# Gathered rows taken in pairs into two running rows of a tile, joined at its end

## The chip, the cores and the metric

The kernel runs on one core of a Trainium2 chip. A core has five engines that run beside each other and meet at semaphores: TensorE (PE, with its weight loads shown as PEld), VectorE (DVE), ScalarE (ACT), GpSimd (POOL) and SyncE (SP). The metric is device microseconds of one execution; the figure compared is the median of several runs.

## What is computed

A graph of 3125 nodes with 256 features each and 103125 edges, which come sorted by their destination node, goes through two layers. Each layer adds a graph step and a linear attention, and then a mixture of eight experts. Cut to what the change touches:

```python
# layer 0: for each node the largest message over its incoming edges
theta_x = (x_dst - x_src) @ theta_w.T + theta_b
phi_x = x_src @ phi_w.T + phi_b
out = jax.ops.segment_max(relu(theta_x + phi_x), dst, num_segments=3125)
# layer 1: for each node the sum of a table's rows, one row for each incoming edge
h_all = jnp.einsum('ni,rio->nro', node_feats, W)      # 8 relations
agg = jax.ops.segment_sum(h_all[src, edge_types], dst, num_segments=3125)
```

The parts of a message that depend on the destination alone are taken out of the maximum, so that both layers come to this: for every node, fetch one 1 KB row of a table in HBM for each incoming edge, and combine the rows (maximum in layer 0, sum in layer 1).

## The kernel before

Nodes are put in order of their number of edges and cut into 25 tiles of 128 nodes, one node for each partition. `STEPS` (line 42) holds the rows that each tile fetches for every one of its nodes: from 45 for tile 0 down to 22 for tile 24, 814 in all. One call of `gather` (line 192; the profile shows all of them on line 193) is an indirect DMA issued by GpSimd that brings one row to each of the 128 partitions.

`edge_pass` (line 1334) does this for a list of groups of tiles. It runs twice: in layer 0 (line 1933, maximum, table `btab`, rows of 264 numbers, all 25 tiles) and in layer 1 (line 2570, sum, table `htab_f`, rows of 256 numbers, 21 tiles; the four tiles named in `EARLY` are summed apart, by `first_group` and `early`). For each tile it cuts the steps into chunks of three or four rows of equal size as far as that goes (`chunks`, line 94), takes a buffer `gt` from the ring `gp` (6 buffers in layer 0, line 1693; 5 in layer 1, line 1987), lets GpSimd gather the rows into it, and lets VectorE fold them: four rows into two by one operation on 512 numbers a partition (line 1356), two into one by one on 256 (line 1356), and the one into the tile's accumulator `acc` by one on 256 (line 1361; line 1359 for a tile's first chunk in layer 0). The accumulators come from the pool `accp` of six buffers.

Behind each chunk `edge_pass` calls jobs from the queue `bg`, as many as a credit allows that grows by 0.9 to 1.3 for each row. These jobs are the rest of the layer: attention, normalization, routing and experts of the tiles whose sums are done (`Fin0` in layer 0, `Group` in layer 1). The order of VectorE's and GpSimd's instructions is the order in which this code is written (`manual_schedule`, lines 1932 and 2568); the orders of the other engines come from a scheduler. So an operation on VectorE that waits for a matrix product holds up the folding of the rows behind it, and GpSimd can only run ahead until the ring `gp` is full.

In layer 0 `seen0` (line 1616) copies a number that comes with each gathered row. In layer 1 a tile's accumulator starts with the row of the node itself: `load_init` (line 2532) brings it one tile ahead, for 16 tiles by a DMA of SyncE from a table `otab` filled earlier, and for the last five tiles in the order of the pass (3, 4, 2, 1, 0; those still in `owns`) by a gather of GpSimd. `begin1` (line 2539) calls it at the start of a tile for the tile that follows.

Between the passes the table `htab_f` is made (line 2047). While it is, `early` gathers rows of the four tiles in `EARLY`, and `add_up` (line 2106) adds a buffer of up to four rows to `sums` by one operation on up to 1024 numbers.

Of the kernel before, what the change touches and what calls it, by code (L numbers as in the profile page):

```python
# [11 lines left out]
F32 = mybir.dt.float32  # L12
# [3 lines left out]
ALU = mybir.AluOpType  # L16
# [4 lines left out]
P = 128  # L21
D = 256
# [19 lines left out]
STEPS = (45, 43, 41, 39, 38, 37, 36, 35, 35, 34, 33, 33, 32, 32, 31, 30, 30, 29, 29, 28, 27, 26, 25, 24, 22)  # L42
# [4 lines left out]
U = STEPS[0] + 1  # L47
# [7 lines left out]
GROUPS = tuple(range(a, b) for a, b in zip(CUTS, CUTS[1:])) + (range(0, 1),)  # L55
# [11 lines left out]
GROUPS1 = tuple(range(b, a) for a, b in zip(CUTS1, CUTS1[1:]))  # L67
GROUPS1 = GROUPS1[2:3] + GROUPS1[:2] + GROUPS1[3:]
# [4 lines left out]
ROW = D + NX  # L73
# [27 lines left out]
def gps_kernel(ctx: ExitStack, tc: tile.TileContext, a, out):  # L101
    nc = tc.nc
    V, S, G, PE = nc.vector, nc.scalar, nc.gpsimd, nc.tensor
# [10 lines left out]
    btab = dram.tile([NPAD, ROW], F32, name="btab")  # L114
# [77 lines left out]
    def gather(dst, table, idx):  # L192
        G.indirect_dma_start(  # L193
            out=dst, out_offset=None, in_=table, in_offset=bass.IndirectOffsetOnAxis(ap=idx, axis=0)
        )
# [758 lines left out]
    with ExitStack() as prx:  # L954
# [48 lines left out]
        for at, t in enumerate(EARLY):  # L1003
            k0 = 0
            while k0 < SOON[t]:
                k1 = k0
# [3 lines left out]
                k0 = k1  # L1010
# [197 lines left out]
        own = pre.tile([P, NV * NT], F32, name="own")  # L1208
# [109 lines left out]
    def fast():  # L1318
        fx = ExitStack()
        ek = fx.enter_context(tc.tile_pool(name="ek", bufs=1))  # L1320
        htab = dram.tile([NPAD, NX * D], F32, name="htab_f")
        otab = dram.tile([NPAD, D], F32, name="otab")
        h_rows = htab.rearrange("n (r d) -> (n r) d", r=NX)
        idx2 = ek.tile([P, NT, U], I32, name="idx2g")
        accp = fx.enter_context(tc.tile_pool(name="accp", bufs=6))
        own_i = ek.tile([P, NT], I32, name="own_i")
        soon = ek.tile([P, len(EARLY), SOONEST], I32, name="soon")
        sure = ek.tile([P, len(EARLY), SOONEST], F32, name="sure")
# [2 lines left out]
        comp = bcast_load("comp", a["comp"], 4 * NX, ek)  # L1331
        br = bcast_load("br0", a["f0_br"], NX, ek)

        def edge_pass(gp, table, wide, idx, op, bg, after, groups, most, pace, own, acc_of, aside, seen=None):


            credit = 0.0
            spill = None
            for g, tiles in enumerate(groups):
                accs = []  # L1340
                left = sum(STEPS[t] for t in tiles)
                for t in tiles:
                    acc = acc_of(t)
                    ids = idx(t)
                    for i, (k0, k1) in enumerate(chunks(STEPS[t], most)):
                        m = k1 - k0
                        gw = gp.tile([P, most, wide], F32, name="gt")
                        gt = gw[:, :, :D]
                        for k in range(k0, k1):
                            gather(gw[:, k1 - 1 - k, :], table, ids[:, U - 2 - k : U - 1 - k])  # L1350
                        if seen is not None:
                            seen(t, i, k0, k1, gw)
                        begins = i == 0 and own is None
                        while m > 1 + begins:
                            h = m // 2
                            V.tensor_tensor(gt[:, :h, :], gt[:, :h, :], gt[:, m - h : m, :], op=op)  # L1356
                            m -= h
                        if begins:
                            V.tensor_tensor(acc, gt[:, 0, :], gt[:, 1, :], op=op)
                        else:  # L1360
                            V.tensor_tensor(acc, own(t) if i == 0 else acc, gt[:, 0, :], op=op)  # L1361
                        if t == 0 and i == 3:
                            V.tensor_tensor(acc[: P // 2, :], acc[: P // 2, :], spill, op=op)

                        rate = min(max(sum(c for c, _ in bg) / left, pace[0]), pace[1])
                        left -= k1 - k0
                        credit = min(credit, 0.0) + rate * (k1 - k0) if bg else 0.0
                        aside()
                        while bg and credit > 0.0:
                            cost, job = bg.popleft()  # L1370
                            job()
                            credit -= cost
                    if t == NT - 1:

                        pj = ps_mm.tile([P, 512], F32, name="mm")
                        PE.matmul(pj[: P // 2, :D], ident[:, P // 2 :], acc, start=True, stop=True)
                        spill = ek.tile([P // 2, D], F32, name="spill")
                        S.copy(spill, pj[: P // 2, :D])
                    accs.append(acc)
                after(g, tiles, accs)  # L1380
# [184 lines left out]
        with ExitStack() as l0x:  # L1565
            l0w = l0x.enter_context(tc.tile_pool(name="l0w", bufs=1))
            idx1, slots_of, sortings = {}, {}, {}
# [123 lines left out]
            b_phi = row_load("b_phi", a["ph_b"], D, l0w)  # L1691
            V.tensor_tensor(b_gnn, b_gnn, b_phi, op=ALU.add)
# [3 lines left out]
            m0 = m0x.enter_context(tc.tile_pool(name="m0", bufs=2))  # L1696

            w_qkv = m0w.tile([P, 2, 3 * D + 2], F32, name="w_qkv")
            S.dma_start(w_qkv[:, :, : 3 * D], a["m0_qkv"].rearrange("(c p) n -> p c n", p=P))
# [2 lines left out]
            for m in range(2):  # L1702
                at = slice(3 * D + m, 3 * D + m + 1)
# [179 lines left out]
            bg = deque(staged(mix_weights(), (3.0, 1.0)))  # L1883
# [39 lines left out]
            fin, waiting = [], []  # L1923
# [7 lines left out]

            with tc.manual_schedule(engines={mybir.EngineType.DVE, mybir.EngineType.Pool}):
                edge_pass(
                    gp, btab[:], ROW, idx1.get, ALU.max, bg, after0, GROUPS, 4, (0.9, 1.3), None,
                    begin0, ahead, seen0,
                )
                while bg:
                    bg.popleft()[1]()
                f0bx.close()
# [14 lines left out]
        with tc.If(again > 0):  # L1954
# [8 lines left out]
            for ts in GROUPS:  # L1963
                k = len(ts)
# [22 lines left out]
        gp = fx.enter_context(tc.tile_pool(name="gp1", bufs=5))  # L1987
        sump = fx.enter_context(tc.tile_pool(name="sump", bufs=1))
        sums = sump.tile([P, len(EARLY), D], F32, name="sums")
        with ExitStack() as tx:  # L1990
# [168 lines left out]
        with ExitStack() as l1x:  # L2159
# [5 lines left out]
            for c in range(2):  # L2165
                d = w_lu[:, c, c * P : (c + 1) * P]
# [15 lines left out]
            fin = l1x.enter_context(tc.tile_pool(name="fin1", bufs=1))  # L2182
# [385 lines left out]
            with tc.manual_schedule(engines={mybir.EngineType.DVE, mybir.EngineType.Pool}):  # L2568
                first_group()
                edge_pass(  # L2570
                    gp, h_rows, D, lambda t: idx2[:, t, :], ALU.add, bg, lambda g, *a: after1(g + 1, *a),
                    GROUPS1[1:], 4, (0.9, 1.3), lambda t: inits[t], begin1, aside,
                )
                while bg:
                    bg.popleft()[1]()
                    flush()
# [3 lines left out]
    with tc.If(unfit < 1):  # L2580
        fast()
# [78 lines left out]
```

## Time and profile before

| what | value |
|---|---|
| median of 5 runs | 2955.13 us (2948.27 to 2980.0) |
| the profiled execution | 2942.73 us, of which the span of instructions is 2941.0 us |
| mean granted TensorE clock | 0.767 |
| busy share of the span | PE 64%, POOL 59%, DVE 43%, ACT 19% |
| first and last gather of layer 0's pass | 99.9 us, 1383.7 us |
| first row gathered early, last gather of layer 1's pass | 1500.0 us, 2853.3 us |

A row of instructions reads: line, engine, operation, what is written and read, count, then busy time and mean duration, then the idle time of the engine just before these instructions and what ended it. An engine that is idle has no instruction whose inputs and buffers are ready; the releaser named is the one that came last. All instructions of VectorE and GpSimd run in the order written. A table by stretches gives for each stretch of the span the busy time of each engine with the number of instructions in brackets, the granted clock, and the share and rate of the DMA engines.

### The profile page before, as it was taken

What the parts mean: (1) busy time and instruction counts of PE and PEld (TensorE: products, weight loads), DVE (VectorE), ACT (ScalarE), POOL (GpSimd) and SP (SyncE); (2) the same over time, 40 slices, a digit from 0 to 9 for tenths busy, and PEclk for the clock granted to TensorE, in tenths of its full rate; (3) what the DMA queues carried; (4) which work ended last, traced back from release to release, by engine and by line L of the source; (5) the groups of instructions that cost most, each with busy time, mean ns of one, the idle gap of its engine ahead of it and who ended that gap; (6) DMA issues with size and microseconds to landing.
All of it is one profiled execution on the core that took longest, in us unless ns stands there. A gap on an engine that the chain in (4) does not pass through costs nothing.

```text
span 2941.0 us, 20996 instructions
## 1 busy us (share of the span) xinstructions
PE 1885.9 (64%) x6033; PEld 1182.2 (40%) x6033; DVE 1256.1 (43%) x3537; ACT 560.2 (19%) x1275; POOL 1726.7 (59%) x1830
## 2 busy tenths in 40 slices
PE   4273667403573655176898349867886796776777
PEld 3131334202341423044443125544454464564666
DVE  8343535536323434244665343434343443343342
ACT  5121211000110101012321112212112122122233
POOL 5566666676657466655036755665666566665560
PEclk9676767655786767577999568877897898887888
DMA  6433333333323233332256632222232222232220
GB/s 191 125 86 89 90 91 101 94 107 108 93 77 105 67 96 87 90 76 76 108 205 218 198 109 76 86 88 77 85 93 87 78 84 84 86 87 74 79 82 15
DMA packets 125962, 290.09 MB, mean 99 GB/s; under 512 B 41386, under 2 KB 63982, under 8 KB 122632
## 3 DMA queue, kind: packets, MB, share of 16 engines
q0 software_dynamic: 83184, 230.02, 27.8%
q1 hardware_dynamic: 38122, 55.88, 5.5%
q10 hardware_dynamic: 4526, 2.71, 0.4%
q8 instruction: 51, 0.84, 0.1%
q14 instruction: 79, 0.65, 0.1%
HBM read 249.07 MB, written 39.41 MB: 98 GB/s over the span
## 4 chain that ended last, share of the span: by engine, by line
PE 27%; issue 8%; another core or an unknown queue 6%; DVE 5%; POOL 3%; ACT 2%; DMA 1%; DVEq 0%; ACTq 0%; POOLq 0%
PE mm L2408 10%; PE py L2439 8%; PE mm L188 6%; POOL gt L193 3%; DVE gt L1356 1%; DMA gt<-htab_f,idx2g 1%; DVE bnst L162 1%; PE mm L2302 1%; PE pt L2378 1%; PE mm L2300 1%; PE pctx L2247 1%; DVE x L2458 1%; PE py L2425 0%; DVE x L2343 0%
## 5 line engine op out<-in xcount | busy, mean ns | idle before, releaser
L193 POOL DMA_INDIRECT gt<-btab,idx x814 | 802.4, 986 | 458.4 <-issue 230.7
L193 POOL DMA_INDIRECT gt<-htab_f,idx2g x742 | 732.2, 987 | 466.8 <-DVE acc L1361 230.5
L2408 PE MATMUL mm<-xT,w 128*128 128x256 f32 (+4 forms) x1408 | 429.6, 457 | 96.8 <-issue 55.1
L2439 PE MATMUL py<-w,hT 128*128 128x256 f32 (+1 forms) x1600 | 404.5, 405 | 84.0 <-issue 43.5
L1356 DVE TENSOR_TENSOR gt<-gt 128x256 f32<-128x256 f32 (+1 forms) x767 | 410.4, 535 | 91.9 <-remote 47.3
L2439 PEld LDWEIGHTS py<-w,hT 128*128 128x128 f32 (+1 forms) x1600 | 316.9, 202 | 163.1 <-issue 85.2
L2408 PEld LDWEIGHTS mm<-xT,w 128*128 128x128 f32 x1408 | 267.4, 217 | 235.7 <-issue 167.5
L2458 DVE SCALAR_TENSOR_TENSOR x<-py,wf,x 128x256 f32<-128x256 f32 x200 | 88.0, 478 | 473.4 <-remote 197.2
L2412 ACT ACTIVATE hT<-mm,b 128x256 f32<-128x256 f32 (+4 forms) x352 | 168.6, 496 | 578.1 <-PE mm L2408 297.6
L188 PE MATMUL mm<-w_rel,xT 128*128 128x512 f32 x400 | 177.1, 601 | 10.0 <-ACT xT L183 9.5
L1532 PE MATMUL mm<-w,hT 128*128 128x256 f32 x400 | 131.6, 489 | 65.3 <-issue 45.8
L1361 DVE TENSOR_TENSOR acc<-acc,gt 128x256 f32<-128x256 f32 x371 | 158.4, 427 | 27.3 <-DVE gt L1356 12.4
L1503 PE MATMUL mm<-xT,w 128*128 128x384 f32 (+2 forms) x320 | 111.1, 513 | 81.4 <-issue 43.1
L1532 PEld LDWEIGHTS mm<-w,hT 128*128 128x128 f32 x400 | 94.1, 246 | 116.4 <-issue 75.8
L188 PE MATMUL mm<-w_qkv,xT 128*128 128x512 f32 (+1 forms) x200 | 104.9, 649 | 38.7 <-ACT vs L1751 38.2
L1863 PE MATMUL pmean<-ones,xt 128*128 128x1 f32 (+1 forms) x100 | 21.2, 316 | 156.5 <-DVE xt L171 156.5
L1503 PEld LDWEIGHTS mm<-xT,w 128*128 128x128 f32 x320 | 69.5, 242 | 122.1 <-issue 64.0
L188 PEld LDWEIGHTS mm<-w_rel,xT 128*128 128x128 f32 x400 | 75.7, 192 | 103.8 <-issue 87.9
L188 PE MATMUL pt<-w_own,xT 128*128 128x256 f32 x100 | 41.7, 552 | 116.8 <-remote 68.9
L193 POOL DMA_INDIRECT gt<-htab_f,soon x72 | 73.0, 1013 | 45.7 <-issue 19.5
L1620 DVE COPY slots<-gt 128x4 f32<-128x4 f32 (+1 forms) x214 | 37.0, 173 | 122.3 <-DMA gt<-btab,idx 118.6
L1863 PEld LDWEIGHTS pmean<-ones,xt 128*128 128x128 f32 (+1 forms) x100 | 21.8, 301 | 166.6 <-DVE xt L171 165.0
(436 smaller groups left out, 2127.9 us busy)
## 6 DMA issues: line engine op xcount, KB each, us to landing
htab_f<-hs SPq DMA_DIRECT2D x25, 1024.0 KB
gt<-btab,idx POOLq DMA_INDIRECT x814
gt<-htab_f,idx2g POOLq DMA_INDIRECT x742
w<-in_f_W_dram SPq DMA_DIRECT2D x20, 512.0 KB
ntab<-x SPq DMA_DIRECT2D x5, 640.0 KB
btab<-bs SPq DMA_DIRECT2D x5, 640.0 KB
x<-in_x_dram SPq DMA_DIRECT2D x4, 640.0 KB
otab<-xn SPq DMA_DIRECT2D x16, 128.0 KB
```

The source lines that it names most:

```text
L188: PE.matmul(ps, lhs[:, c, t * P : (t + 1) * P], w[:, c, :], start=start and c == 0, stop=stop and c == 1)
L193: G.indirect_dma_start(out=dst, out_offset=None, in_=table, in_offset=bass.IndirectOffsetOnAxis(ap=idx, axis=0))
L1356: V.tensor_tensor(gt[:, :h, :], gt[:, :h, :], gt[:, m - h : m, :], op=op)
L1361: V.tensor_tensor(acc, own(t) if i == 0 else acc, gt[:, 0, :], op=op)
L1503: PE.matmul(ph[:, :n], w1[:, i, c, f * P : (f + 1) * P], xT[:, c, at0 : at0 + n], start=(c == 0), stop=(c == 1),)
L1532: PE.matmul(py[:, i * D : (i + 1) * D], hTs[i][:, f, j * P : (j + 1) * P], w2[:, i, f, :], start=False, stop=(f == FC - 1), skip_group_che ...
L1620: V.tensor_copy(slots_of[t][:, U - 1 - k1 : U - 1 - k0], gw[:, : k1 - k0, D])
L1863: PE.matmul(pmean[0][:, c : c + 1], xt_tok[:r, t, c * P : (c + 1) * P], ones[:r, 0:1], start=(t in (1, SEEN + 1) and c == 0), stop=(t in ( ...
L2408: PE.matmul(ph[:, :n], w1s[e][:, c, f * P : (f + 1) * P], xT[:, c, at0 : at0 + n], start=(c == 0), stop=(c == 1),)
L2412: S.activation(hT[:, f, :n], ph[:, :n], AF.Gelu, bias=b1[:, e, f : f + 1])
L2439: PE.matmul(py[:r, j * D : (j + 1) * D], hT[:, f, at : at + r], w2s[e][:, f, :], start=(f == 0), stop=(f == FC - 1),)
L2458: V.scalar_tensor_tensor(d, y, wf[:r, t, e : e + 1], d, op0=ALU.mult, op1=ALU.add)
```

## The change

In `edge_pass` a tile now has two running rows, `run`, in place of one accumulator. The first two rows (in layer 1 the node's own row and the first gathered row) go straight into `run`. Every further chunk has four rows, the last one what is left, and is taken in pairs: one operation on 512 numbers adds two gathered rows to the two running rows. At the end of the tile, behind the jobs of its last chunk, one operation on 256 numbers joins the two running rows into `acc`, which is only then taken from `accp`.

```diff
-        accp = fx.enter_context(tc.tile_pool(name="accp", bufs=6))
+        accp = fx.enter_context(tc.tile_pool(name="accp", bufs=5))
...
-                    acc = acc_of(t)
+                    run = run_of(t)
+                    two = run[:, :, :D]
...
-                    for i, (k0, k1) in enumerate(chunks(STEPS[t], most)):
-                        m = k1 - k0
-                        gw = gp.tile([P, most, wide], F32, name="gt")
-                        gt = gw[:, :, :D]
-                        for k in range(k0, k1):
-                            gather(gw[:, k1 - 1 - k, :], table, ids[:, U - 2 - k : U - 1 - k])
+                    n0 = 1 if owned else 2
+                    for k in range(n0):
+                        fetch_row(run[:, 1 - k, :], k)
+                    if seen is not None:
+                        seen(t, 0, 0, n0, run)
+                    for i, k0 in enumerate(range(n0, STEPS[t], 4)):
+                        k1 = min(k0 + 4, STEPS[t])
+                        gw = gp.tile([P, 4, wide], F32, name="gt")
+                        for a in range(k0, k1, 2):
+                            b = min(a + 2, k1)
+                            at = slice(k1 - b, k1 - a)
+                            for k in range(a, b):
+                                fetch_row(gw[:, k1 - 1 - k, :], k)
+                            d = two[:, : b - a, :]
+                            V.tensor_tensor(d, d, gw[:, at, :D], op=op)
                         if seen is not None:
-                            seen(t, i, k0, k1, gw)
-                        begins = i == 0 and own is None
-                        while m > 1 + begins:
-                            h = m // 2
-                            V.tensor_tensor(gt[:, :h, :], gt[:, :h, :], gt[:, m - h : m, :], op=op)
-                            m -= h
-                        if begins:
-                            V.tensor_tensor(acc, gt[:, 0, :], gt[:, 1, :], op=op)
-                        else:
-                            V.tensor_tensor(acc, own(t) if i == 0 else acc, gt[:, 0, :], op=op)
+                            seen(t, i + 1, k0, k1, gw)
...
+                    acc = accp.tile([P, D], F32, name="acc")
+                    V.tensor_tensor(acc, two[:, 0, :], two[:, 1, :], op=op)
```

`run` has two buffers in each layer. In layer 1 `load_init` writes the own row into the `run` of the tile that follows; `add_up` takes at most two rows in one operation:

```diff
-                return accp.tile([P, D], F32, name="acc")
+                return l0w.tile([P, 2, ROW], F32, name="run", bufs=2)
...
-                inits[t] = accp.tile([P, D], F32, name="acc")
+                inits[t] = fin.tile([P, 2, D], F32, name="run", bufs=2)
                 if t in owns:
-                    gather(inits[t], h_rows, own_i[:, t : t + 1])
+                    gather(inits[t][:, 0, :], h_rows, own_i[:, t : t + 1])
                 else:
-                    nc.sync.dma_start(inits[t], otab[t * P : (t + 1) * P, :])
+                    nc.sync.dma_start(inits[t][:, 0, :], otab[t * P : (t + 1) * P, :])
...
-                    e = slice(es[k0], es[k1 - 1] + 1)
-                    V.tensor_tensor(sums[:, e, :], sums[:, e, :], gt[:, e, :], op=ALU.add)
+                    for a in range(k0, k1, 2):
+                        e = slice(es[a], es[min(a + 1, k1 - 1)] + 1)
+                        V.tensor_tensor(sums[:, e, :], sums[:, e, :], gt[:, e, :], op=ALU.add)
```

A row of biases, `b_phi`, moves to a pool that is given up earlier. The number of gathers stays as it was.

More of the change, by code (lines that the diff above doesn't have):

```diff
@@ L1332, in fast, with edge_pass @@
         br = bcast_load("br0", a["f0_br"], NX, ek)
-        def edge_pass(gp, table, wide, idx, op, bg, after, groups, most, pace, own, acc_of, aside, seen=None):
+        def edge_pass(gp, table, wide, idx, op, bg, after, groups, pace, owned, run_of, aside, seen=None):
             credit = 0.0
@@ L1342, in edge_pass, with fetch_row @@
                 for t in tiles:
-                    acc = acc_of(t)
+                    run = run_of(t)
+                    two = run[:, :, :D]
                     ids = idx(t)
-                    for i, (k0, k1) in enumerate(chunks(STEPS[t], most)):
-                        m = k1 - k0
-                        gw = gp.tile([P, most, wide], F32, name="gt")
-                        gt = gw[:, :, :D]
-                        for k in range(k0, k1):
-                            gather(gw[:, k1 - 1 - k, :], table, ids[:, U - 2 - k : U - 1 - k])
-                        if seen is not None:
-                            seen(t, i, k0, k1, gw)
-                        begins = i == 0 and own is None
-                        while m > 1 + begins:
-                            h = m // 2
-                            V.tensor_tensor(gt[:, :h, :], gt[:, :h, :], gt[:, m - h : m, :], op=op)
-                            m -= h
-                        if begins:
-                            V.tensor_tensor(acc, gt[:, 0, :], gt[:, 1, :], op=op)
-                        else:
-                            V.tensor_tensor(acc, own(t) if i == 0 else acc, gt[:, 0, :], op=op)
+                    def fetch_row(dst, k):
+                        gather(dst, table, ids[:, U - 2 - k : U - 1 - k])
@@ L1362, in edge_pass @@
                         if t == 0 and i == 3:
-                            V.tensor_tensor(acc[: P // 2, :], acc[: P // 2, :], spill, op=op)
+                            V.tensor_tensor(two[: P // 2, 0, :], two[: P // 2, 0, :], spill, op=op)
                         rate = min(max(sum(c for c, _ in bg) / left, pace[0]), pace[1])
-                        left -= k1 - k0
-                        credit = min(credit, 0.0) + rate * (k1 - k0) if bg else 0.0
+                        n1 = k1 - (k0 if i else 0)
@@ L1368, in edge_pass @@
+                        left -= n1
+                        credit = min(credit, 0.0) + rate * n1 if bg else 0.0
                         aside()
@@ L1690, in fast @@
             S.dma_start(b_mix, a["m0_bout"].rearrange("(o n) -> o n", o=1))
-            b_phi = row_load("b_phi", a["ph_b"], D, l0w)
-            V.tensor_tensor(b_gnn, b_gnn, b_phi, op=ALU.add)
             gp = l0x.enter_context(tc.tile_pool(name="gp0", bufs=6))
@@ L1696, in fast @@
             m0 = m0x.enter_context(tc.tile_pool(name="m0", bufs=2))
+            b_phi = row_load("b_phi", a["ph_b"], D, m0w)
+            V.tensor_tensor(b_gnn, b_gnn, b_phi, op=ALU.add)
             w_qkv = m0w.tile([P, 2, 3 * D + 2], F32, name="w_qkv")
@@ L1933, in fast @@
                 edge_pass(
-                    gp, btab[:], ROW, idx1.get, ALU.max, bg, after0, GROUPS, 4, (0.9, 1.3), None,
+                    gp, btab[:], ROW, idx1.get, ALU.max, bg, after0, GROUPS, (0.9, 1.3), False,
                     begin0, ahead, seen0,
@@ L2571, in fast @@
                     gp, h_rows, D, lambda t: idx2[:, t, :], ALU.add, bg, lambda g, *a: after1(g + 1, *a),
-                    GROUPS1[1:], 4, (0.9, 1.3), lambda t: inits[t], begin1, aside,
+                    GROUPS1[1:], (0.9, 1.3), True, begin1, aside,
                 )
```

## The prediction

> **What bounds the kernel now.** I began with the costliest groups of the page. The two edge passes are gathers on POOL: 814 in layer 0, 742 in layer 1.
>
> ```profile
> L193 POOL DMA_INDIRECT gt<-btab,idx x814 | 802.4, 986 | 458.4 <-issue 230.7
> L193 POOL DMA_INDIRECT gt<-htab_f,idx2g x742 | 732.2, 987 | 466.8 <-DVE acc L1361 230.5
> ```
>
> A gather is 0.99 us busy and some 0.3 us of issue: 1.28 us at best. The idle time beyond issue is split by the waits of POOL over the whole run (us in total, times, longest):
>
> ```profile
> POOL gt L193 <- issue: 449.5, 1448, 4.2
> POOL gt L193 <- DVE acc L1361: 356.7, 76, 18.8
> ```
>
> So POOL stands 357 us, in 76 pieces, because the ring of `gt` buffers is full and line 1361, a chunk's last fold, has not freed one. Why DVE is late is in its own waits:
>
> ```profile
> DVE x L2458 <- remote: 197.2, 15, 24.7
> DVE x L2458 <- PE mm L2408: 136.6, 11, 25.7
> DVE x L2458 <- PE py L2439: 122.9, 48, 10.9
> ```
>
> The folds stand in line behind jobs that wait for PE. A table by stretches shows that no engine is full (PE, PEld, DVE, ACT, POOL busy; clock, DMA):
>
> ```profile
> 95.00:560.00 465.00, 280.76 (x720) 144.20 (x720) 205.17 (x701) 86.00 (x313) 291.81 (x300) 0.69 0.36 96
> 560.00:1360.00 800.00, 366.31 (x1031) 224.69 (x1031) 310.55 (x899) 75.40 (x158) 519.91 (x525) 0.66 0.34 92
> 1620.00:2430.00 810.00, 592.22 (x1919) 374.79 (x1918) 319.53 (x767) 152.15 (x265) 500.73 (x503) 0.80 0.32 95
> 2430.00:2790.00 360.00, 262.77 (x967) 198.03 (x966) 140.74 (x369) 81.61 (x153) 217.42 (x223) 0.83 0.28 82
> ```
>
> From 560 to 1360 us POOL with its issue time is at 525 x 1.28 = 672 of 800 us and PE at 46%: gathers pace that stretch. From 1620 on PE is at 73% and POOL at 78 to 80% with issue: PE and POOL hold each other up through DVE's order. DVE, 38 to 44% busy, is not full anywhere; its time counts where it stands between them.
>
> **Part 1, fewer operations on VectorE.** Its groups by shape:
>
> ```profile
> L1356 DVE TENSOR_TENSOR gt<-gt 128x512 f32<-128x512 f32 x322 | 220.5, 685 | 23.9 <-DMA gt<-htab_f,idx2g 23.6
> L1356 DVE TENSOR_TENSOR gt<-gt 128x256 f32<-128x256 f32 x445 | 189.9, 427 | 68.0 <-remote 47.3 <-issue 5.0 <-DVE gt L1356 3.7
> L1361 DVE TENSOR_TENSOR acc<-acc,gt 128x256 f32<-128x256 f32 x371 | 158.4, 427 | 27.3 <-DVE gt L1356 12.4 <-remote 1.7 <-issue 1.3
> ```
>
> With 25 more of 427 ns (line 1359) these are 322 long and 841 short operations. After, counted from `STEPS`: layer 0 has 375 long and 39 short (the 25 joins among them), layer 1 333 and 30 (21 joins). 386 operations go; as many numbers are added as before, and 256 of them cost 685 - 427 = 258 ns, so each operation saved is worth 169 ns. In sum 322 x 0.685 + 841 x 0.427 = 579.7 us become 708 x 0.685 + 69 x 0.427 = 514.4: 65 us less. At most all of it is on the path (-65), at least none, where DVE would wait for PE anyway. I take DVE's busy share of the span, 43%: -28 us.
>
> **Part 2, the ring holds more rows.** Chunks are 814/214 = 3.80 rows in layer 0 and 696/182 = 3.82 in layer 1; now they are 4 except a tile's last. Six buffers reach 1.2 rows further, five 0.9: 1.5 and 1.1 us at 1.25 us a gather. That shortens a wait of POOL only where POOL is the bound, so mainly from 560 to 1360 us, with about 25 waits on DVE: at most 37 us. I take half, -20; the ends are 0 and, if every wait in both passes shrank so, 33 x 1.5 + 50 x 1.1 = -105.
>
> **Part 3, a new wait on GpSimd.** Before, an own row went into one of six accumulators and its five gathers waited for nothing (issue alone). Now the next tile's `run` is the buffer of the tile just ended, and is free when DVE has joined that tile. In the built order each of these five gathers waits for DVE, and the chunks behind it carry no wait on DVE until the ring is used up again: POOL stands until DVE has caught up. Queued behind it on POOL are all gathers of the next tile. The 16 other own rows wait on SP, a tile ahead, with nothing urgent behind. What one such boundary looks like now, in the timeline (start, duration):
>
> ```profile
> 2518.24 0.95 POOL L193 DMA_INDIRECT acc<-htab_f,own_i  x1 [0.30 <-issue]
> 2519.50 0.95 POOL L193 DMA_INDIRECT gt<-htab_f,idx2g  x1 [0.30 <-issue]
> ...
> 2531.21 0.88 DVE L2458 SCALAR_TENSOR_TENSOR x<-py,wf,x 128x256 f32<-128x256 f32 x2 [17.06 <-remote]
> ...
> 2533.87 0.94 POOL L193 DMA_INDIRECT gt<-htab_f,idx2g  x1 [5.92 <-DVE acc L1361]
> ...
> 2535.12 1.15 POOL L193 DMA_INDIRECT gt<-htab_f,idx2g  x1 [0.31 <-issue]
> ...
> 2536.57 0.94 POOL L193 DMA_INDIRECT gt<-htab_f,idx2g  x1 [0.30 <-issue]
> 2537.06 0.43 DVE L1361 TENSOR_TENSOR acc<-acc,gt 128x256 f32<-128x256 f32 x1
> ```
>
> The own row of tile 4 is asked for at 2518.2; the last fold of tile 6 ends at 2537.5. POOL would stand those 19.3 us. At the other four places the same distance is 24.1, 22.2, 25.2 and 24.8 us: 116 in all, the upper end. But POOL waits 71 us on DVE between 2430 and 2790 anyway, and with an empty ring it would not. What is certainly new is DVE's idle time after the join: four gathers (own row, first row, first pair) of 1.25 us and a landing. A landing is 2.8 us (a gather ended at 2071.64 and the fold that waited for it began at 2074.48). 7.8 us, five times 39; PE works on queued products meanwhile, which DVE then need not wait for. I take 5 us each, +25; ends 0 and +116.
>
> **Part 4, longer operations against gathers.** The gather at 2535.12, over a fold, took 1.15 us, its neighbours 0.94. Over 1628 gathers the mean of 0.986 against 0.95 is 59 us. Weighing each operation by its square (chance of a hit times what is left of it), 322 x 0.469 + 841 x 0.182 = 304 becomes 708 x 0.469 + 69 x 0.182 = 345, 13% more: +8. `add_up` goes the other way: 23 operations of 1221 ns become 46 of 685, +3 us of DVE beside PE's table products (nothing on the path; 3 us if that cover is gone), and gathers are held up for shorter: -3. Together +5; ends -10, the whole of `add_up`'s hits gone, and +20. The Trainium skill, "SBUF — State Buffer", section "SBUF: two separate sides", speaks against this change: a VectorE operation with two SBUF inputs and a GpSimd operation that reads SBUF lock each other out for a whole instruction. By that rule alone, with a gather's start equally likely at every moment of 1.25 us, the squares above would cost 304/2.5 = 122 us before and 138 after, an estimate of +16; the rows show half as much.
>
> **What else moves.** The copies of `seen0` come behind the pair, 0.17 us each, and 11 more of them (25 for the first rows, 14 chunks fewer), 2 us beside POOL's 1.28 a row. In layer 0 the gathers into `run` wait for no DVE. PE's and ACT's orders are drawn up anew by the scheduler, which no row prices; I allow 15 us either way, most of the longest wait of POOL on a fold (18.8).
>
> **Sum.** -28 - 20 + 25 + 5 = -18 us on the profiled execution of 2942.73: 2925. That execution lies 12.4 us under the median of the runs shown, which the forecast keeps: 2955.13 - 18 = 2937 us.
>
> **Rivals.** *The own-row waits decide (slower).* If POOL's standing is not made good, because DVE, emptied at each boundary, then follows the gathers at 1.28 us a row with no ring to bridge PE's waits, the full 116 us count: -28 - 20 + 116 + 5 = +73, 3028 us. It decides from (28 + 20 - 5)/5 = 8.6 us a boundary; against it stands that the ring is full at each of these places, so DVE's side sets the pace. *DVE's time is on the path nearly whole (faster).* The full 65, and 37 from the ring, against 25 and 5: -72, 2883 us. For it: the 76 waits all end with line 1361, whose chain of 0.685 + 2 x 0.427 becomes 2 x 0.685. Against: DVE waits 457 us for PE at line 2458. *Nothing comes of it.* PE's and POOL's rates hold both passes and saved DVE time becomes longer waits at line 2458: 2945 to 2965.
>
> **How the numbers follow.** The forecast has 0.45, its own range 2910 to 2965; the own-row rival 0.22; the fast rival 0.22; nothing 0.11. A measurement of this kernel can tell about 1% (30 us) from no change. Faster by over 1% (below 2926): the fast rival and 0.14 of the forecast, 0.36. Slower by over 1% (above 2984): most of the own-row rival and 0.04 of the rest, 0.24. Within: 0.40. The range takes the fast rival's middle and half the way to the slow one's end: 2880 to 3000.
>
> **What would show it.** Right: 708 operations of 512 numbers near 685 ns; waits of POOL on a line 1361 replaced by fewer on the pair's line; five waits of `run` on the join, 15 to 25 us each, and few other waits of POOL from 2430 on. Wrong: those five under 8 us, or POOL's other waits unchanged beside them; gathers above 1.02 us in the mean; a stretch from 560 to 1360 us that is no shorter. An order of PE that leaves it idle longer before line 2408 would upset all of this.

## The result and the profile after

| | median | lowest to highest |
|---|---|---|
| before | 2961.69 us of 94 runs | 2932.22 to 2987.4 |
| after | 2969.16 us of 52 runs | 2944.93 to 2988.63 |
| ratio | 1.003, 95% interval 1.0016 to 1.0044 | |

The change makes the kernel 0.3% slower, some 9 us, where 18 us less were forecast. The profiled execution took 2946.65 us (span 2944.9, clock 0.767, as before), 3.9 us more than that of before. Its groups and its waits of GpSimd over the whole run:

```profile
L193 POOL DMA_INDIRECT gt<-btab,idx x764 | 756.3, 990 | 372.6 <-issue 206.3 <-DVE slots L1628 76.4 <-DVE rs L1863 30.5
L193 POOL DMA_INDIRECT gt<-htab_f,idx2g x721 | 712.9, 989 | 422.0 <-issue 202.0 <-DVE run L1364 189.4 <-DVE sums L2123 17.4
L193 POOL DMA_INDIRECT run<-htab_f,own_i x5 | 4.7, 947 | 82.9 <-DVE acc L1380 65.1 <-issue 17.7
L1364 DVE TENSOR_TENSOR run<-run,gt 128x512 f32<-128x512 f32 x708 | 489.0, 691 | 300.9 <-DMA gt<-btab,idx 147.6 <-DMA gt<-htab_f,idx2g 92.5 <-remote 28.0
```
```profile
POOL gt L193 <- DVE run L1364: 198.6, 64, 20.9
POOL gt L193 <- DVE slots L1628: 76.4, 22, 14.7
POOL run L193 <- DVE acc L1380: 65.1, 4, 22.2
```

The 708 operations are there at 691 ns, and a gather is as long as it was (0.99 us). GpSimd's waits for buffers of rows fell from 357 us on line 1361 and 21 on line 1359 to 199 + 76. The third line of each fence is new: five own-row gathers, before which GpSimd stands 82.9 us. (One of the five, 17.73 us, is put down to "issue". VectorE's join ended at 2639.40 there and the gather began at 2641.15, so all but the last 1.75 us of it are the same wait.) Their own lines in the timeline, with the idle time before each in brackets:

```profile
2438.48 0.95 POOL L193 DMA_INDIRECT run<-htab_f,own_i  x1 [18.69 <-DVE acc L1380]
2498.27 0.95 POOL L193 DMA_INDIRECT run<-htab_f,own_i  x1 [6.03 <-DVE acc L1380]
2574.80 0.94 POOL L193 DMA_INDIRECT run<-htab_f,own_i  x1 [18.26 <-DVE acc L1380]
2641.15 0.95 POOL L193 DMA_INDIRECT run<-htab_f,own_i  x1 [17.73 <-issue]
2723.48 0.95 POOL L193 DMA_INDIRECT run<-htab_f,own_i  x1 [22.17 <-DVE acc L1380]
```

Where the 4 us of the traces come from is seen by the first gathers of the tiles (before, after, difference):

| moment | before | after | difference |
|---|---|---|---|
| last gather of layer 0 | 1383.7 | 1346.6 | -37.1 |
| first gather of layer 1's pass | 1631.4 | 1594.6 | -36.7 |
| first gather of tile 5, layer 1 | 2400.9 | 2360.7 | -40.1 |
| last gather of layer 1 | 2853.3 | 2861.8 | +8.6 |
| end of the span | 2941.0 | 2944.9 | +4.0 |

So layer 0 won, layer 1 up to tile 5 added almost nothing, and from tile 5 to the last gather, where the five own rows lie, 48.7 us were lost (452.4 us became 501.1). VectorE's waits in just that stretch, from the first gather of tile 5 to the last gather (before, then after; us, times, longest):

```profile
DVE x L2458 <- remote: 95.4, 7, 24.7
DVE gt L1356 <- DMA gt<-htab_f,idx2g: 2.3, 1, 2.3
```
```profile
DVE x L2467 <- remote: 141.0, 8, 26.5
DVE run L1364 <- DMA gt<-htab_f,idx2g: 73.9, 28, 8.3
```

Before, VectorE found its rows in place: it waited for a gather once. After, it waits 73.9 us for gathers, in 28 pieces, and its waits on lines 2458 and 2450 (now 2467 and 2459), which take products of TensorE, are no shorter than before: 222 us, where they were 192. The timeline of VectorE at the last of the five places shows how this looks:

```profile
2722.80 0.41 DVE L1380 TENSOR_TENSOR acc<-run 128x256 f32<-128x256 f32 x1
2730.11 0.69 DVE L1364 TENSOR_TENSOR run<-run,gt 128x512 f32<-128x512 f32 x1 [6.90 <-DMA gt<-htab_f,idx2g]
2732.87 0.69 DVE L1364 TENSOR_TENSOR run<-run,gt 128x512 f32<-128x512 f32 x1 [2.07 <-DMA gt<-htab_f,idx2g]
...
2735.19 0.69 DVE L1364 TENSOR_TENSOR run<-run,gt 128x512 f32<-128x512 f32 x1 [0.84 <-DMA gt<-htab_f,idx2g]
2737.68 0.69 DVE L1364 TENSOR_TENSOR run<-run,gt 128x512 f32<-128x512 f32 x1 [1.80 <-DMA gt<-htab_f,idx2g]
```

After the join at 2722.80 the ring is empty. VectorE waits 6.90 us for the first pair, and then for each of the next three too, 1 to 2 us a time, since it is faster than the gathers and nothing is in store. This ends when its next instruction, which takes a product of TensorE, starts only at 2748.84, after 10.46 us of idle time, while the gathers run on and fill the ring. At the five places the waits for gathers come to 8.7, 15.2, 25.3, 13.1 and 11.6 us.

### The profile page after: what moved, and what is told of

Its sections match the earlier page's. It is cut to its first block, busy times and chain, and to the rows that moved or that the text cites. A ratio compares the mean times of both kernels' runs of the same rounds, so it can differ in the third digit from the quotient of the medians.

```text
span 2944.9 us, 20602 instructions
## 1 busy us (share of the span) xinstructions
PE 1843.1 (63%) x6033; PEld 1163.3 (40%) x6033; DVE 1202.5 (41%) x3185; ACT 556.3 (19%) x1273; POOL 1729.9 (59%) x1830
## 4 chain that ended last, share of the span: by engine, by line
PE 25%; another core or an unknown queue 11%; issue 7%; DVE 5%; POOL 2%; ACT 2%; DMA 1%; ACTq 0%; DVEq 0%; POOLq 0%
PE mm L2417 9%; PE py L2448 7%; PE mm L188 5%; POOL gt L193 2%; DVE run L1364 2%; PE mm L2311 1%; DVE bnst L162 1%; PE mm L2309 1%; PE pt L2387 1%; DVE x L2467 1%; PE pctx L2256 0%; ACT hT L2421 0%; PE py L2434 0%; DVE x L2352 0%
## 5 line engine op out<-in xcount | busy, mean ns | idle before, releaser
L193 POOL DMA_INDIRECT gt<-btab,idx x764 | 756.3, 990 | 372.6 <-issue 206.3
L193 POOL DMA_INDIRECT gt<-htab_f,idx2g x721 | 712.9, 989 | 422.0 <-issue 202.0
L1364 DVE TENSOR_TENSOR run<-run,gt 128x512 f32<-128x512 f32 x731 | 498.7, 682 | 306.7 <-DMA gt<-btab,idx 150.9
L2417 PE MATMUL mm<-xT,w 128*128 128x256 f32 (+4 forms) x1408 | 414.0, 448 | 98.8 <-DVE x L2317 42.1
L2448 PE MATMUL py<-w,hT 128*128 128x256 f32 (+1 forms) x1600 | 411.1, 408 | 98.0 <-issue 73.4
L2417 PEld LDWEIGHTS mm<-xT,w 128*128 128x128 f32 x1408 | 263.5, 214 | 226.8 <-issue 123.7
L1511 PE MATMUL mm<-xT,w 128*128 128x384 f32 (+2 forms) x320 | 103.6, 489 | 44.7 <-DMA w<-in_f_W_dram 25.6
L188 PE MATMUL mm<-w_qkv,xT 128*128 128x512 f32 (+1 forms) x200 | 92.7, 588 | 33.7 <-issue 33.7
L1511 PEld LDWEIGHTS mm<-xT,w 128*128 128x128 f32 x320 | 66.1, 230 | 81.9 <-issue 31.3
L188 PEld LDWEIGHTS pt<-w_own,xT 128*128 128x128 f32 x100 | 23.0, 255 | 143.4 <-DVE acc L1853 81.2
L193 POOL DMA_INDIRECT run<-btab,idx x50 | 49.7, 994 | 45.2 <-DVE idx L1615 20.1
```

The source lines that it names most:

```text
L188: PE.matmul(ps, lhs[:, c, t * P : (t + 1) * P], w[:, c, :], start=start and c == 0, stop=stop and c == 1)
L193: G.indirect_dma_start(out=dst, out_offset=None, in_=table, in_offset=bass.IndirectOffsetOnAxis(ap=idx, axis=0))
L1364: V.tensor_tensor(d, d, gw[:, at, :D], op=op)
L1511: PE.matmul(ph[:, :n], w1[:, i, c, f * P : (f + 1) * P], xT[:, c, at0 : at0 + n], start=(c == 0), stop=(c == 1),)
L2417: PE.matmul(ph[:, :n], w1s[e][:, c, f * P : (f + 1) * P], xT[:, c, at0 : at0 + n], start=(c == 0), stop=(c == 1),)
L2448: PE.matmul(py[:r, j * D : (j + 1) * D], hT[:, f, at : at + r], w2s[e][:, f, :], start=(f == 0), stop=(f == FC - 1),)
```

## The experiments

Theory A: the five own-row waits cost what the passes win. Theory B, the rival: the loss is in TensorE's new order and its clock. The runs fell on chips of two kinds: on some the kernel before takes 2477 to 2481 us, on others 2962 to 2983, as in the result (there VectorE often waits for TensorE). So each ratio is to the kernel before on the same chip, and times of versions are compared on one chip alone.

### On chips where before takes some 2480 us

**e1, three run buffers in layer 1**: the own row has a free buffer.

```diff
-                inits[t] = fin.tile([P, 2, D], F32, name="run", bufs=2)
+                inits[t] = fin.tile([P, 2, D], F32, name="run", bufs=3)
```

> The changed kernel with three buffers of run in layer 1 in place of two, so that the five gathers of an own row no longer wait for the join of the tile before. Theory A (the own-row waits cost what the passes win): in the changed kernel's trace layer 0 ends its gathers 37 us earlier than before, tile 5 of layer 1 begins 40 us earlier, and the last gather is 9 us later, so about 49 us are lost at the five own rows. Without them 2969 - 45 = about 2920 to 2930 us, ratio 0.986 to 0.990, and no wait of a run gather above 1 us. Theory B (PE's new order and clock from 2430 us on are what costs, and the own-row waits only take the place of waits for the ring): as the changed kernel, ratio 1.000 to 1.005.

**e7, the own row asked for seven chunks into the tile**, with two buffers.

```diff
+                if put_off and tick[0] >= put_off[0]:
+                    load_init(put_off[1])
+                    put_off.clear()
...
+                if i < len(order1) and order1[i] in owns:
+                    put_off[:] = [tick[0] + 7, order1[i]]
```

> The changed kernel with run's two buffers as they are, but the own row of the next tile is asked for seven chunks into a tile and not at its start, when the join of the tile before is long done. Theory A: as with three buffers, ratio 0.986 to 0.990, 2920 to 2930 us. Theory B: 1.000 to 1.005. If three buffers help and this does not, the buffer did something else than free the own rows.

**e3, pairs in layer 0 only**: layer 1 runs the old folds on six accumulators.

```diff
-                edge_pass(
+                edge_chain(
                     gp, h_rows, D, lambda t: idx2[:, t, :], ALU.add, bg, lambda g, *a: after1(g + 1, *a),
```

> Pairs and running rows in layer 0 alone; layer 1 folds chunks into accumulators as before (its own rows in six buffers). Theory A: layer 0 keeps its 37 us and nothing is lost in layer 1: ratio 0.986 to 0.990, 2920 to 2930 us. Theory B: the gain of layer 0 in one trace is within the scatter of single executions, ratio 0.997 to 1.003.

**e4, pairs in layer 1 only**: the kernel before, with the new function for layer 1 and two run buffers.

```diff
-                edge_pass(
+                edge_pairs(
                     gp, h_rows, D, lambda t: idx2[:, t, :], ALU.add, bg, lambda g, *a: after1(g + 1, *a),
```

> Pairs and running rows in layer 1 alone, with run's two buffers; layer 0 folds as before. Theory A: no gain of layer 0, the own-row waits in full, a few us of VectorE saved: ratio 1.012 to 1.017, 2998 to 3012 us. Theory B: 1.000 to 1.005.

Measured on one chip (before 2477.0 us): e1 0.9941 (0.9927 to 0.9954), e7 0.995 (0.9936 to 0.9963), e3 0.9949 (0.9935 to 0.9963), e4 1.0088 (1.0074 to 1.0102). Both ways of taking the wait away make the change a gain, and layer 1 alone loses 23 us (2499.58 - 2477.0): theory A by its signs. Its sizes had been forecast from the trace of a chip of the other kind, and all four came out smaller. As e1 and e3 agree, pairs in layer 1 without the wait win nothing that can be seen here.

**e9, the changed kernel again, e10, three buffers again, e5 and e8** ran side by side on another chip of this kind (before 2480.39 us).

> The changed kernel itself, beside the kernel before on whichever chip this lands on. Theory A (the five own-row waits cost what the passes win): 0.4 to 1.0% slower than the version with three run buffers on the same chip, so 1.000 to 1.005 of before, with five waits of run on the join that add up to 60 to 120 us. Theory B (PE's new order and clock): within 0.2% of the version with three buffers.

> Three run buffers in layer 1, beside the changed kernel on the same chip. Theory A: 0.990 to 0.996 of before if gathers pace the run as on the chip of the first four runs; on a chip where the kernel before takes some 2950 us, where the five waits cost 50 to 60 us in the trace, 0.982 to 0.988. Theory B: as the changed kernel, 1.000 to 1.005.

e5 changes only where layer 0's chunks are cut:

```diff
+def four_each(n, most):
+    return [(k, min(k + most, n)) for k in range(0, n, most)]
...
-                    for i, (k0, k1) in enumerate(chunks(STEPS[t], most)):
+                    for i, (k0, k1) in enumerate(cut(STEPS[t], most)):
```

> The kernel before, with only one thing changed: layer 0 cuts its tiles into chunks of four rows as far as they go, instead of chunks of nearly equal size, with the old folds. It is the part of the prediction called the ring that holds more rows, alone. If that part carries the gain of layer 0: 0.994 to 0.997 where before takes some 2480 us, 0.988 to 0.993 where it takes some 2950. If the fewer operations carry it: 0.998 to 1.002.

e8 undoes the split of `add_up`:

```diff
-                    for a in range(k0, k1, 2):
-                        e = slice(es[a], es[min(a + 1, k1 - 1)] + 1)
+                    e = slice(es[k0], es[k1 - 1] + 1)
```

> The changed kernel with the split of add_up taken back: its additions cover up to 1024 numbers each again. If the split is what keeps the gathers of the stage between the passes short: their mean goes from some 970 ns to 1020 or more, and the run is 3 to 10 us slower than the changed kernel. If it is worth nothing: within 0.1% of the changed kernel.

Measured: e9 1.0039 (1.0027 to 1.0051), e10 0.9939 (0.9917 to 0.996), so the waits cost 24.4 us (2489.74 - 2465.34); in the trace of e9 GpSimd stands 29.4 us before the five own rows, where 60 to 120 were expected. e5 1.0011 (0.9997 to 1.0024): a fuller ring brings nothing where gathers pace the pass. e8 1.0064 (1.0045 to 1.0083): the split is worth 6.7 us against e9. Why, the gathers between the passes show (e9, then e8; shortest, median and longest of 72):

```profile
L193 POOL DMA_INDIRECT gt<-htab_f,soon x72: 940/946/1453, 1281.8 to 1405.5; - x72
```
```profile
L193 POOL DMA_INDIRECT gt<-htab_f,soon x72: 941/947/1955, 1282.0 to 1409.2; - x72
```

Their mean goes from 993 to 1031 ns. The first gather of layer 1's pass is 3.6 us later in e8 (1410.4 against 1406.8), and some 3 us more come with the first 40 gathers behind it, which `add_up` sums too.

**e11, the split alone, e12, `add_up` by single rows, e13, the own row three chunks late** (before 2481.36 us). e11 is the kernel before with e8's removed lines; e12 is three buffers with slices of one row; e13 is e7 with 3 for 7.

> The kernel before, with only the split of add_up: additions of at most 512 numbers each, which cover no more than two rows. If it is the split, and not the pairs, that wins between the passes: 0.995 to 0.998 of before, and the mean of the 72 gathers into soon's buffers 20 to 80 ns shorter. If the split gains only together with the pairs: 0.999 to 1.001.

> The version with three run buffers, with add_up by single rows, so 256 numbers an operation. If shorter operations of VectorE let gathers pass sooner here, 1 to 4 us under three buffers; if the extra operations (some 427 ns for each half instead of 690 for both) cost on VectorE what the gathers win, the same within 0.1%, 0.993 to 0.995 of before.

> The changed kernel with two run buffers, where the own row of the next tile is asked for three chunks of four rows into the tile instead of at its first row. Theory A: the wait is gone where VectorE catches up with the join within twelve rows, some 15 us, so on a chip with waits of 4 to 9 us each it runs like three buffers (0.993 to 0.996), and on one with waits of 18 to 22 us it keeps a small part of them. Theory B: as the changed kernel, 1.002 to 1.005.

Measured: e11 0.998 (0.9971 to 0.9989), the split wins 4 us by itself. e13 0.994 (0.9925 to 0.9956): twelve rows of delay are enough, and GpSimd's time before the five own rows is 1.5 us. e12 0.9926 (0.9911 to 0.9941), 4 us under e13, which had the longer additions, but the two intervals overlap: not told apart. Three buffers with the longer additions, with which e12 was to be compared, did not run on this chip.

### On chips where before takes 2963 to 2983 us

**e14, each row folded by itself**, in the version with three buffers.

```diff
-                            d = two[:, : b - a, :]
-                            V.tensor_tensor(d, d, gw[:, at, :D], op=op)
+                            for q in range(b - a):
+                                d = two[:, q, :]
+                                V.tensor_tensor(d, d, gw[:, k1 - b + q, :D], op=op)
```

> The version with three run buffers, with each pair added as two operations of 256 numbers in place of one of 512: some 708 operations more of VectorE, 708 x (2 x 0.427 - 0.690) = 116 us more of its time, in the same order. If 43% of VectorE's time lies on the path, as the prediction took it: 50 us slower than three buffers, 1.010 to 1.018 of before. If gathers pace the passes: within 5 us of three buffers, 0.992 to 0.997, or even a little faster, since shorter operations hold gathers up for less.

**e15, e16 and e17**: the kernel before, the changed kernel and three buffers, with more work for TensorE in layer 1

```diff
-                            for f in range(FC):
+                            for f in [*range(FC)] * (2 if e % 2 == 0 else 1):
```

and with `outputs_a` in layer 0 computed twice.

> The kernel before, with TensorE given more to do: the products of outputs_a in layer 0, and those of outputs for four of the eight experts in layer 1, are computed twice in a row (the same result). 1168 matmuls of 0.39 us are 450 us of TensorE more, part of it in its idle time. It is the base of the next two: expected 150 to 400 us longer than before, with VectorE waiting for TensorE and GpSimd waiting for folds 200 us or more, as on the chip where before took 2955 us.

> The changed kernel with the same load on TensorE. Theory A: the five own-row waits grow from 29 us to between 60 and 120 us, and the run is 15 to 60 us slower than the next one, with three buffers. Theory B: as the next one, within 0.2%. Against the loaded kernel before: 0.99 to 1.01 by A.

> Three run buffers with the same load on TensorE. Theory A: 0.98 to 0.99 of the loaded kernel before, since the first pass wins and nothing is lost at the own rows. If TensorE sets both passes under this load, 0.995 to 1.0 of the loaded kernel before, and then the loaded changed kernel is no slower either, as GpSimd's waits are made good.

Measured on one chip (before 2982.79 us): e15 1.0439 (1.0397 to 1.048), e16 1.0574 (1.0524 to 1.0623), e17 1.0472 (1.0425 to 1.0519). The waits cost 33 us (3151.77 - 3118.35), with 88.9 us of standing before the own rows, as theory A has it. The other half of its forecast missed: three buffers are no faster than the loaded kernel before, and the changed kernel is 1.2% slower than it, not within 1%. The second forecast of e17 missed too, by which the loaded changed kernel would then lose nothing. Under this load the passes win nothing, but standing still costs; that it is TensorE that paces them is argued, not shown (it is busy 69% of the span of e17). e15 grew by 133 us, a little under its forecast. e14, 0.998 (0.9948 to 1.0013), came out just above the second of its forecasts; its reading is below.

**e18, three buffers, e19, the changed kernel, and e20, chunks of four** (e1, e9 and e5 again) on one chip of this kind (before 2962.8 us): the measurement that settles the question.

> Three run buffers in layer 1, hoped for the chip on which the kernel before takes some 2960 us. Theory A: the trace of the changed kernel there lost 49 to 60 us from tile 5 to the end, against 40 us won up to it, so 0.982 to 0.988 of before. If most of that stretch was TensorE's new order (theory B): 0.997 to 1.005. On the loaded TensorE three buffers were 33 us better than two, which by itself would make 0.990 to 0.994.

> The changed kernel on the same chip, for the difference to three buffers. Theory A: 1.000 to 1.006 of before, 30 to 55 us more than three buffers. Theory B: within 6 us of three buffers.

> The kernel before with layer 0 in chunks of four, on the same chip: the ring that holds more rows, alone. If it carries the 37 us that the changed kernel's first pass won there: 0.986 to 0.992 of before. If the fewer operations carry them: 0.998 to 1.003.

Measured: e18 0.9854 (0.9817 to 0.9891), e19 0.9993 (0.9964 to 1.0022), e20 0.9921 (0.989 to 0.9952). By these ratios two buffers instead of three cost 41 us ((0.9993 - 0.9854) x 2962.8). The waits from tile 5 to the last gather, first of three buffers (442 us), then of the changed kernel (499 us):

```profile
POOL gt L193 <- DVE run L1364: 71.2, 16, 7.8
POOL gt L193 <- DVE rsh L2363: 9.6, 2, 6.0
...
DVE run L1364 <- DMA gt<-htab_f,idx2g: 1.7, 1, 1.7
```
```profile
POOL run L193 <- DVE acc L1380: 63.9, 4, 22.2
POOL gt L193 <- DVE run L1364: 56.1, 10, 8.2
POOL gt L193 <- DVE rsh L2363: 4.0, 1, 4.0
...
DVE run L1364 <- DMA gt<-htab_f,idx2g: 74.4, 28, 8.4
```

In the changed kernel GpSimd stands 81.7 us before the five own rows (17.8 of it under the name of "issue"), and its other waits in the stretch shrink only from 80.8 to 60.1 us. Five times 0.3 us is plain issue: 81.7 - 1.5 - 20.7 = 59.5 us are new, and the stretch is 57 us longer. (This execution had reached tile 5 13.5 us sooner than that of e18, so that the ends lie 44 us apart.) VectorE's waits for gathers go from 1.7 to 74.4 us, 14.9 a boundary.

The two traces also bear on theory B. The recorded matrix products stand in the same order in both but for one place, from 2460.6 to 2499.9 us of e19, within tile 6, where 38 of them come later than in e18. At the first gathers of tiles 5, 6, 3, 4, 2, 1 and 0 the lag of e19 behind e18 is -13.5, 3.7, 2.4, 17.8, 25.5, 42.9 and 39.1 us: over tile 6 it does not grow, and with each of three own rows 15 us or more come to it. The granted clock in this stretch was 0.83 in e18 and 0.79 in e19, and TensorE was busy for 328 and 339 us, so by this difference the clock may have a part of some 11 of the 57 us. On the chip of e9 and e10 it has none: 0.89 and 0.90, TensorE busy for 305 and 306 us, and the waits still cost 24 us.

Three buffers beat the kernel before on each of the three chips where they ran without the load, by 1.5% here and 0.6% on the other two, and the changed kernel wherever both ran.

## Why the prediction was wrong, point by point

**The sign: the step that failed is Part 3, by its size.** It had the mechanism, the five places and the queue that stands behind them. It took 5 us a boundary, 25 in all, out of a range of 0 to 116. The runs put it at 41 us on the chip of e18 and e19, at 24.4 where gathers pace everything, at 33 with TensorE loaded; the trace of the result lost 48.7 us in that stretch. With 48.7 in place of 25 the forecast's sum is +6 us; the result is +9 (interval 5 to 13). Two sentences were at fault. "POOL waits 71 us on DVE between 2430 and 2790 anyway, and with an empty ring it would not": it still does. From tile 5 to the last gather its other waits on VectorE went from 98 us (78.5 on line 1361, 16.7 on line 2354, the rest small) to 61.5 only. The standing before the five own rows is 81.4 us beyond plain issue, 36 are given back so, and 45 stay, of 48.7 lost. The ring is full again within the same tile, some 30 gathers after the own row (the fourth is followed by a wait of 7.3 us at 2685.7). And "what is certainly new is DVE's idle time after the join", 7.8 us each: that is only the first gap (6.90 in the timeline above). VectorE then follows the gathers pair by pair, and 73.9 / 5 = 14.8 us a boundary is what it waits in the mean. "PE works on queued products meanwhile, which DVE then need not wait for" holds in part: on the chip of e18 and e19 VectorE's waits on lines 2467 and 2459 in the stretch fell from 243 to 218 us, a third of the 73 us that it lost to gathers; between the two traces of the result they did not fall at all (192, then 222 us). The price lies between the forecast's and that of the rival "the own-row waits decide", whose mechanism this is and whose 8.6 us a boundary was the right point: 41 / 5 = 8.2 makes e19 a draw, and 48.7 / 5 = 9.7 in the recorded trace a loss.

**The other parts were right in sum.** Without the waits the change should bring -28 - 20 + 5 = -43 us. Three buffers measured 2962.8 x (0.9854 - 1) = -43 us, interval -54 to -32. That the sum meets the middle so closely is partly luck, since the working of Part 1 does not hold (below). That is the kind of chip the forecast was made for; on the other kind the same version brings -15 (e10).

**Part 2, the fuller ring (-20):** e20 gives 2962.8 x (0.9921 - 1) = -23 us, interval -33 to -14, and nothing where GpSimd hardly waits for folds (e5). Right in size, and bound to that condition, which Part 2 named: waits on folds. That the fuller ring is what won is argued from the edit, not seen in a trace: the only trace of e20 is its slowest execution (2969.79 us), and GpSimd's waits on folds are as long there as before (355.5 us on line 1365).

**Parts 1 and 4, fewer operations and longer gathers (-28 + 5):** what e20 leaves to e18 is 20 us, against 23, with the split of `add_up` in it (4 us by itself in e11). The two were not separated. VectorE's busy time over the span fell by 53.6 us (1256.1 to 1202.5), where Part 1 forecast 65 for its folds alone. But the working of Part 1 was not sound: it valued an operation saved at 169 ns, from durations. In a backlog, starts count. Chunks of four as they follow each other in VectorE's timeline, before, and two chunks after:

```profile
2060.57 1.14 DVE L1356 TENSOR_TENSOR gt<-gt 128x512 f32<-128x512 f32 x2
2061.75 0.42 DVE L1361 TENSOR_TENSOR acc<-acc,gt 128x256 f32<-128x256 f32 x1
2062.10 1.14 DVE L1356 TENSOR_TENSOR gt<-gt 128x512 f32<-128x512 f32 x2
```
```profile
2712.05 2.86 DVE L1364 TENSOR_TENSOR run<-run,gt 128x512 f32<-128x512 f32 x4
```

A chunk began every 1.53 us, and now takes 2 x (2.86 - 0.69) / 3 = 1.45: 0.08 us saved, not 2 operations of 685 for one of 685 and two of 427, 0.17. The next chunk's first operation starts before the last fold's 0.42 us are over.

e14 was meant to price this and did not, since it did not add 116 us to VectorE: its busy time is 1218 us, against 1201 in e18. Two operations of 256 that do not depend on each other start 0.335 us apart (the median of some 1000 starts in its trace), so a pair done as two takes 0.67 us where one of 512 takes 0.72. What it did change are the gathers of both passes (e18, then e14):

```profile
L193 POOL DMA_INDIRECT gt<-btab,idx x764 | 752.3, 985 | 363.3 <-issue 205.6 <-DVE slots L1628 68.0 <-DVE s_sm L1459 14.4
L193 POOL DMA_INDIRECT gt<-htab_f,idx2g x721 | 713.5, 990 | 444.3 <-DVE run L1364 204.9 <-issue 199.9 <-DVE sums L2123 17.2
```
```profile
L193 POOL DMA_INDIRECT gt<-btab,idx x764 | 762.1, 997 | 394.3 <-issue 207.9 <-DVE slots L1629 71.5 <-DVE run L1365 24.0
L193 POOL DMA_INDIRECT gt<-htab_f,idx2g x721 | 730.8, 1014 | 465.7 <-DVE run L1365 231.4 <-issue 196.9 <-DVE sums L2124 18.3
```

762.1 - 752.3 + 730.8 - 713.5 = 27 us more of gathers. The two ran on two chips of one kind; on e14's chip the loaded version with three buffers (e17) has gathers of 988 and 991 ns in the mean in these two groups, so the chip is hardly the cause. The share of VectorE's folds on the path (43% in Part 1) therefore stays open.

**Part 4** had gathers right: 0.99 us in both passes, 1534.6 us in all before and 1540.4 after (+6, forecast +8), and in the stage between, 1013 ns became 968, 72 x 45 = 3 us. That layer 1's pass starts 3.6 us later in e8 shows that these stand on the path there. The longest gathers, 1955 ns beside additions of 1222 and 1453 beside additions of 690, are 1.01 and 0.51 us over the common 0.945. This agrees with the rule of the Trainium skill ("SBUF — State Buffer", "SBUF: two separate sides") that one side holds the other up for a whole instruction at most: the excess stays below the length of the VectorE operation in both. Weighing operations by their squares does not fit e14, though: 1439 short ones have a smaller sum of squares than 708 long ones, and longer gathers.

**PE's new order (15 us either way), theory B,** is not needed for the sign: the changed kernel without the waits is 41 us faster, with an order on TensorE that differs from the changed kernel's at one place in layer 1 only, and the lag grows at the own rows. How much a single trace may mislead is seen in layer 0: its last gather lay 37 us ahead of before in the recorded trace, but e18 and e19, whose first pass is the same code, ended it 11 us apart (1378.1 and 1366.7).

**What would show it:** the 708 operations and the waits on the pair's line came as named. Of the five waits four were within 15 to 25 us, one was 6.0. "Few other waits of POOL from 2430 on" failed, and this was the sign of a larger price.

## What to carry to other kernels

When an in-order engine waits for a consumer to finish a whole tile, the ring between them runs dry, and the price is not the first gap alone: count the consumer's idle time until the store is full again as its upper end (14.8 us a boundary on the chips of e19 and of the result, where 8 to 10 were lost), and do not credit the producer's usual waits, which return once the ring has filled. A buffer that is taken early and freed late (here a running row asked for one tile ahead, freed by the join) needs one more copy than the chain suggests, or has to be asked for later: one more buffer turned this change from a draw into -1.5% on one kind of chip and from +0.4% into -0.6% on the other, where a delay of twelve rows did the same. In a backlog, value a saved operation by the distance of starts, not by durations.

## What was not expected of the hardware

The same kernel took 2477 us on one chip and 2983 on another; on the first kind none of the waits of VectorE that the profile puts down to "remote" is left (197 us on line 2458 alone in the profile before) and gathers set the pace, so an edit's worth depends on the chip (three buffers: 0.6% and 1.5%). VectorE starts an independent operation of 256 numbers 0.335 us after the last one, though each is recorded with 0.42 us, and twice as many short operations came with gathers that were 12 to 24 ns longer in the mean, not shorter (e18 and e14, on two chips of one kind).
